# Other places for h's parts in the second half's row of operands, in an LSTM step on one core

## The chip, the core and the metric

The kernel runs on one core of a Trainium2 chip. The metric is the device time of one execution in microseconds (us). The core has TensorE (PE; its weight loads are shown apart as PEld), VectorE (DVE), ScalarE (ACT), GpSimd (POOL) and SyncE (SP); each works through its own queue in order and waits on semaphores that the others raise.

## The reference

One LSTM layer over a sequence, added to its input: 16 sequences (N), 512 steps (T), width 512 (D and H).

```python
xW = jnp.einsum('ntd,dg->ntg', x, Wx) + b
def step(carry, xw_t):
    prev_h, prev_c = carry
    a = xw_t + prev_h @ Wh
    i, f, o = sigmoid of a[:, :H], a[:, H:2H], a[:, 2H:3H];  g = tanh(a[:, 3H:])
    next_c = f * prev_c + i * g
    next_h = o * jnp.tanh(next_c)
    return ((next_h, next_c), next_h)
out = x + hs          # hs: the next_h of all steps; h0 = cond_1024, c0 = 0
```

The inputs are float32. Step t + 1 needs h of step t, so the loop over t can't be opened up.

## The kernel before

**Halves.** The hidden units are taken in two halves, a (h = 0) and b (h = 1). Each half has its own gates bank in PSUM, its own operand tiles and its own chain of elementwise work, and the two chains are interleaved so that TensorE has products of one half to do while the other half's gates are worked on.

**Products.** The product of h with Wh is made of float16 products. Wh is split once into three float16 tensors, `wq[0]`, `wq[1]` and `wq[2]`. In each step h is split into float16 parts that lie in one row of operands per half, `parts[h][t % 2]`, two times five slots of 16 columns (N): p1 is h scaled and rounded, copy is p1 once more, p2 is the remainder of h after p1, p2r is a second combination of the two. A product takes two neighbouring slots as its stationary operand of 32 columns, 16 of them for the main part of the sum and 16 for a part that is later divided by LO = 4096. Which of the two 16 rows has which meaning changes with the parity of t. There are three kinds: q1 (with `wq[0]`) takes p1 and p2, q2 (with `wq[1]`) takes copy and p2r, q3 (with `wq[2]`) takes p1 and a slot that stays zero. `products(t, i, kh, h)` issues one of them: qi for the half kh of h's rows and the half h of the gates, as eight matmuls of 128 x 32 weights against 256 columns, two contraction chunks (cc) times four column groups (j).

**Names.** "q3ba" is q3 with half b's operands into half a's gates. The order on TensorE is written out by hand in STEP_PE, and that on VectorE and ScalarE in STEP; every engine keeps exactly this order:

```python
STEP_PE = "q3aa q3ab q1ab q1aa q2aa q3ba q1ba q2ba q2bb q1bb q2ab q3bb x0 x1"
```

x0 and x1 are `project`, the float32 projections of a later pair of steps (L165).

**The chain of a half.** When the last product into gates a (q2ba) is done, turn_a and turno_a transpose the gates (L224), fold_a and foldo_a join the two parts (L231), ScalarE makes the tanh and sigmoids (L258, L260, L264), scale_a multiplies o's by a scale (L266), mix_a and cell_a make the new cell (L268, L274), ctanh_a its tanh (L276). Then come the parts: p1 on VectorE (L284), h on VectorE (L278), copy on ScalarE (L288, it reads p1), p2 on VectorE (L290), rem on VectorE (L294), p2r on VectorE (L298). Half b's chain is the same and begins after q3bb. `slots(t, h, kind)` gives where a part is written for step t + 1: kind 0 is p1, 1 is p2, 2 is copy, 3 is p2r.

**Around it.** `seed` puts the projection into the gates bank two steps ahead (ScalarE, L175), and every second step has the residual (L325 on VectorE, L326 on POOL) and the next transposition of x (L161).

Of the kernel before, what the change touches and what calls it, by code (L numbers as in the profile page):

```python
# [31 lines left out]
def lstm_residual(ctx: ExitStack, tc: tile.TileContext, x, h0, wx, wh, b, out):  # L32
# [78 lines left out]

    parts = [
        [const.tile([P, 2, 5 * N], HP, tag=f"parts{h}{i}", name=f"parts{h}{i}") for i in range(2)]
        for h in range(2)
# [65 lines left out]
    def products(t, i, kh, h):  # L182
        g = gates[h][t % 2]
        a = parts[kh][t % 2]
        k = ((1, 3, 0), (0, 3, 1))[t % 2][i - 1]
        for cc in range(2):
            for j in range(NJ):
                nc.tensor.matmul(  # L188
                    g[j * Q : (j + 1) * Q, :GU],
                    lhsT=a[:, cc, k * N : (k + 2) * N],  # L190
                    rhs=wq_j[i - 1][:, 2 * kh + cc, h, j],
                    start=False,
                    stop=False,
                    skip_group_check=True,
                )
# [43 lines left out]

    def slots(t, h, kind):  # L240

        k = ((1, 2, 3, 4), (1, 0, 4, 3))[(t + 1) % 2][kind]
        return parts[h][(t + 1) % 2][:, :, k * N : (k + 1) * N]

    def hl(t, h):
# [2 lines left out]
    def act(t, op, h):  # L248
# [22 lines left out]
        elif op == "cell":  # L271
            gc[h] = state.tile([P, 2, 2 * N], FP, tag=f"gc{h}", name=f"gc{h}_{t}")
            pr = v["pr", h]
            nc.vector.tensor_tensor(gc[h][:, 1], pr[:, 0], pr[:, 1], ALU.add)  # L274
        elif op == "ctanh":
            nc.scalar.activation(new("tch", t, h, [P, 2 * N]), gc[h][:, 1], AF.Tanh)  # L276
        elif op == "h":
            nc.vector.scalar_tensor_tensor(  # L278
                hl(t, h), two(v["os", h]), LO, two(v["tch", h]), ALU.mult, ALU.mult
            )  # L280
        elif t + 1 == T:
            return
        elif op == "p1":
            nc.vector.tensor_tensor(  # L284
                slots(t, h, 0), two(v["os", h]), two(v["tch", h]), ALU.mult
            )
        elif op == "copy":
            nc.scalar.copy(slots(t, h, 2), slots(t, h, 0))  # L288
        elif op == "p2":
            nc.vector.scalar_tensor_tensor(  # L290
                slots(t, h, 1), slots(t, h, 0), -LO, hl(t, h), ALU.mult, ALU.add
            )
        elif op == "rem":
            nc.vector.scalar_tensor_tensor(  # L294
                new("rem", t, h, [P, 2, N]), slots(t, h, 0), -LO, hl(t, h), ALU.mult, ALU.add
            )
        else:
            nc.vector.scalar_tensor_tensor(  # L298
                slots(t, h, 3), v["rem", h], 2.0, slots(t, h, 1), ALU.mult, ALU.subtract
            )  # L300
# [184 lines left out]
    for t in range(T):  # L485
# [5 lines left out]
        for op in STEP_PE.split():  # L491
            if op[0] == "x":
                if q < NP:
                    project(q, 2 * half + int(op[1:]))
            elif t:
                products(t, int(op[1]), "ab".index(op[2]), "ab".index(op[3]))
            elif op[1] == "3":
                first_products("ab".index(op[2]), "ab".index(op[3]), hT0)

        for op in STEP.split():  # L500
            name, h = op.split("_")
# [47 lines left out]
```

## Time and profile before

| | |
|---|---|
| median of 3 runs | 2294.73 us (2294.44 to 2298.69) |
| profiled execution | 2294.09 us |
| its span | 2291.7 us |
| granted TensorE clock | 0.999 |
| PE busy | 2249.4 us, 57445 matmuls |
| PEld busy | 1572.7 us |
| DVE, ACT, POOL busy | 1952.7, 1838.1, 127.2 us |
| products, L188 | 49056 matmuls, mean 273 ns each |
| projections, L165 | 8192 matmuls, mean 593 ns each |

The span is the profiled execution from its first to its last instruction. Matmuls are pipelined and the ends of them are modelled, so several are in flight at a time and the mean of one is not the time that it adds. PEld is the loading of weights, which goes on beside matmuls. The chain of waits is followed back from the last instruction: at each step to what released it, or to the instruction before it on its engine. An idle time is put down to what ended it. EVENT_SEMAPHORE is an instruction that only waits.

### The profile page before, as it was taken

The numbers are of one execution on the slowest core, as the hardware profiler recorded it, in microseconds if no ns is written. First come the engines' busy times: TensorE is split into PE (matmuls) and PEld (weight loads), VectorE is DVE, ScalarE is ACT, GpSimd is POOL, SyncE is SP. The second block draws the span as 40 slices with busy tenths as digits, with TensorE's granted clock in tenths as the row PEclk, the third lists the DMA queues.
The fourth block names the chain that finished last, engine by engine and source line by source line (L and its number), as shares of the span: only waits on it lengthen the run. The fifth ranks groups of instructions, "written<-read, shape, count | busy, mean of one in ns | idle before, by whom it ended". The sixth has DMA issues, their size and how long they took to land.

```text
span 2291.7 us, 137735 instructions
## 1 busy us (share of the span) xinstructions
PE 2249.4 (98%) x57445; PEld 1572.7 (69%) x57445; DVE 1952.7 (85%) x11813; ACT 1838.1 (80%) x7959; POOL 127.2 (6%) x281
## 2 busy tenths in 40 slices
PE   4999999999999999999999999999999999999997
PEld 2677766777766777777666777776677777666775
DVE  5888888888888888888888888888888888888887
ACT  5888888888888888888888888888888888888887
POOL 1000000000000000000000000000000000000000
PEclk9999999999999999999999999999999999999999
DMA  7000000100100001000001001010000010010000
GB/s 166 13 21 15 22 18 17 22 15 20 22 14 22 22 13 22 21 14 22 17 18 22 15 20 22 13 22 22 13 22 19 17 22 18 17 22 15 20 18 12
DMA packets 85005, 51.10 MB, mean 22 GB/s; under 512 B 17104, under 2 KB 82720, under 8 KB 83872
## 3 DMA queue, kind: packets, MB, share of 16 engines
q1 hardware_dynamic: 83008, 37.82, 7.6%
q8 instruction: 452, 7.41, 1.4%
q0 software_dynamic: 928, 2.37, 0.5%
q10 hardware_dynamic: 448, 2.13, 0.4%
q14 instruction: 169, 1.38, 0.2%
HBM read 25.47 MB, written 16.78 MB: 18 GB/s over the span
## 4 chain that ended last, share of the span: by engine, by line
PE 98%; DMA 2%; DVE 0%; issue 0%; ACTq 0%; POOLq 0%; POOL 0%; SPq 0%
PE gates L188 59%; PE xb L165 38%; DMA wh_sb<-in_L_cond_Wh_dram 1%; DMA xs<-in_x_dram 0%; DMA wx_sb<-in_L_cond_Wx_dram 0%; PE gates L201 0%; PE xb L374 0%; ACTq L134 0%; DVE gt L224 0%; DVE preo L231 0%; DVE pre L231 0%; DVE parts L284 0%; DVE gto L224 0%; POOLq L544 0%; POOL ob L326 0%
## 5 line engine op out<-in xcount | busy, mean ns | idle before, releaser
L188 PEld LDWEIGHTS <-parts 128*32 128x32 f16 x49056 | 1307.1, 96 | 368.8 <-DVE parts L284 298.8
L188 PE MATMUL gates<-wq,parts 128*32 128x256 f16 x49056 | 1449.2, 273 | 4.2 <-DVE parts L284 4.2
L165 PE MATMUL xb<-wx_sb,xT 128*32 128x512 f32 x8192 | 977.1, 593 | 22.5 <-DMA wx_sb<-in_L_cond_Wx_dram 22.5
L224 DVE STREAM_TRANSPOSE gt<-gates 128x192 f32<-128x192 f32 x1024 | 391.7, 383 | 229.9 <-PE gates L188 170.7
L165 PEld LDWEIGHTS xb<-wx_sb,xT 128*32 128x32 f32 x8192 | 264.6, 110 | 327.5 <-issue 303.5
L258 ACT ACTIVATE gc<-pre 128x32 f32<-128x32 f32 x1022 | 234.7, 230 | 274.7 <-DVE pre L231 261.9
L175 ACT ACTIVATE gates<-xb,mask 128x256 f32<-128x256 f32 x1024 | 450.3, 440 | 2.1 <-PE xb L165 2.1
L266 ACT ACTIVATE os<-so,sc 128x32 f32<-128x32 f32 x1024 | 329.1, 321 | 16.6
L288 ACT COPY parts<-parts 128x32 f16<-128x32 f16 x1022 | 214.4, 210 | 131.7 <-DVE parts L284 131.7
L231 DVE SCALAR_TENSOR_TENSOR pre<-gt 128x96 f32<-128x96 f32 x1024 | 253.6, 248 | 0.0
L260 ACT ACTIVATE sif<-pre 128x64 f32<-128x64 f32 x1024 | 245.7, 240 | 0.0
L326 POOL TENSOR_TENSOR ob<-hb,xs 128x128 f32<-128x128 f32 x256 | 117.1, 457 | 2146.0 <-DVE hb L325 1732.5
L224 DVE STREAM_TRANSPOSE gto<-gates 128x64 f32<-128x64 f32 x1024 | 229.6, 224 | 0.0
L276 ACT ACTIVATE tch<-gc 128x32 f32<-128x32 f32 x1024 | 226.8, 221 | 0.3
L298 DVE SCALAR_TENSOR_TENSOR parts<-rem,parts 128x32 f16<-128x32 f32 x1022 | 196.3, 192 | 35.5
L264 ACT ACTIVATE so<-preo 128x32 f32<-128x32 f32 x1024 | 226.4, 221 | 0.0
L231 DVE SCALAR_TENSOR_TENSOR preo<-gto 128x32 f32<-128x32 f32 x1024 | 192.6, 188 | 17.5
L290 DVE SCALAR_TENSOR_TENSOR parts<-parts,hist 128x32 f16<-128x32 f16 x1022 | 192.0, 188 | 17.7
L268 DVE TENSOR_TENSOR pr<-sif,gc 128x64 f32<-128x64 f32 x1022 | 204.2, 200 | 0.0
L284 DVE TENSOR_TENSOR parts<-os,tch 128x32 f16<-128x32 f32 x1022 | 196.5, 192 | 0.0
L274 DVE TENSOR_TENSOR gc<-pr 128x32 f32<-128x32 f32 x1024 | 192.1, 188 | 0.0
L278 DVE SCALAR_TENSOR_TENSOR hist<-os,tch 128x32 f32<-128x32 f32 x1024 | 188.7, 184 | 0.3 <-ACT tch L276 0.3
(47 smaller groups left out, 730.8 us busy)
## 6 DMA issues: line engine op xcount, KB each, us to landing
xs<-in_x_dram SPq DMA_DIRECT2D x512, 32.0 KB, 2.0
out_dram<-ob SPq DMA_DIRECT2D x504, 32.0 KB, 1.7
wh_sb<-in_L_cond_Wh_dram ACTq DMA_DIRECT2D x4, 512.0 KB, 13.4
wh_sb<-in_L_cond_Wh_dram SPq DMA_DIRECT2D x4, 512.0 KB, 13.1
wx_sb<-in_L_cond_Wx_dram POOLq DMA_DIRECT2D x8, 256.0 KB, 9.5
wx_sb<-in_L_cond_Wx_dram SPq DMA_DIRECT2D x8, 256.0 KB, 6.8
bias<-in_L_cond_b_dram POOLq DMA_DIRECT2D x8, 32.0 KB, 13.4
out_dram<-ob SPq DMA_DIRECT2D x8, 24.0 KB, 1.6
```

Source lines behind the costliest of these rows:

```text
L165: nc.tensor.matmul(xb[q % NXB][j * Q : (j + 1) * Q], lhsT=xT[q][:, c], rhs=wx_j[:, c, j], start=False, stop=(c == NK - 1), skip_group_chec ...
L175: nc.scalar.mul(gates[h][t % 2][:, :GU].rearrange("p (g u) -> p g u", g=G), xb[t // 2 % NXB].rearrange("p (g h u) -> p h g u", g=G, h=2)[: ...
L188: nc.tensor.matmul(g[j * Q : (j + 1) * Q, :GU], lhsT=a[:, cc, k * N : (k + 2) * N], rhs=wq_j[i - 1][:, 2 * kh + cc, h, j], start=False, st ...
L224: nc.vector.transpose(gt.rearrange("p b m -> p (b m)"), gates[h][t % 2][:, b0 * Q : b1 * Q])
L231: nc.vector.scalar_tensor_tensor(pre.rearrange("p g (c n) -> p (g c) n", c=2), gt[:, :, (1 - t % 2) * N : (2 - t % 2) * N], 1.0 / LO, gt[: ...
L258: nc.scalar.activation(gc[h][:, 0], v["pre", h][:, 0], AF.Tanh)
L260: nc.scalar.activation(new("sif", t, h, [P, 2, 2 * N]), v["pre", h][:, 1:3], AF.Sigmoid)
L264: nc.scalar.activation(new("so", t, h, [P, 2 * N]), v["preo", h][:, 0], AF.Sigmoid)
L266: nc.scalar.mul(new("os", t, h, [P, 2 * N]), v["so", h], S[h])
L268: nc.vector.tensor_tensor(new("pr", t, h, [P, 2, 2 * N]), v["sif", h], gc[h], ALU.mult)
L276: nc.scalar.activation(new("tch", t, h, [P, 2 * N]), gc[h][:, 1], AF.Tanh)
L288: nc.scalar.copy(slots(t, h, 2), slots(t, h, 0))
```

## The change

For half b the parts get other slots, and the products with half b's operands read from other slots. For half a everything stays. In terms of slots 0 to 4 of half b (the place that stays zero is written 0):

| | slots before | slots after | q1, q2, q3 begin at, before | after |
|---|---|---|---|---|
| operands of even t | 0, p1, p2, copy, p2r | p1, p2, 0, copy, p2r | 1, 3, 0 | 0, 3, 2 |
| operands of odd t | p2, p1, 0, p2r, copy | p2, p1, p2r, copy, 0 | 0, 3, 1 | 0, 2, 3 |

So q1 and q2 take the same pairs as before, and q3 of half b takes copy and the zero slot where it took p1 and the zero slot.

```diff
+    AT = (((1, 3, 0), (0, 3, 1)), ((0, 3, 2), (0, 2, 3)))
+    SLOTS = (((1, 2, 3, 4), (1, 0, 4, 3)), ((0, 1, 3, 4), (1, 0, 3, 2)))
...
     def products(t, i, kh, h):
         g = gates[h][t % 2]
         a = parts[kh][t % 2]
-        k = ((1, 3, 0), (0, 3, 1))[t % 2][i - 1]
+        k = AT[kh][t % 2][i - 1]
...
     def slots(t, h, kind):
 
-        k = ((1, 2, 3, 4), (1, 0, 4, 3))[(t + 1) % 2][kind]
+        k = SLOTS[h][(t + 1) % 2][kind]
         return parts[h][(t + 1) % 2][:, :, k * N : (k + 1) * N]
```

## The prediction

> **What bounds the kernel now.** I read the page first: busy shares, then the chain that ended last.
>
> ```profile
> PE 2249.4 (98%) x57445; PEld 1572.7 (69%) x57445; DVE 1952.7 (85%) x11813; ACT 1838.1 (80%) x7959; POOL 127.2 (6%) x281
> PE 98%; DMA 2%; DVE 0%; issue 0%; ACTq 0%; POOLq 0%; POOL 0%; SPq 0%
> PE gates L188 59%; PE xb L165 38%; DMA wh_sb<-in_L_cond_Wh_dram 1%; DMA xs<-in_x_dram 0%; DMA wx_sb<-in_L_cond_Wx_dram 0%; PE gates L201 0%; PE xb L374 0%; ACTq L134 0%; DVE gt L224 0%; DVE preo L231 0%; DVE pre L231 0%; DVE parts L284 0%; DVE gto L224 0%; POOLq L544 0%; POOL ob L326 0%
> ```
>
> The chain is TensorE alone: products (L188) and projections (L165). So time can only come from the spacing of matmuls, and VectorE (85%) and ScalarE (80%) matter only by when they release TensorE. Next the waits: which have TensorE on the left.
>
> ```profile
> PEld L188 <- DVE parts L284: 298.8, 511, 1.7
> DVE gt L224 <- PE gates L188: 170.7, 450, 0.6
> ACT parts L288 <- DVE parts L284: 131.7, 511, 0.3
> ```
>
> The 298.8 us are no lost time: that weight load is q3aa's, it starts 144 ns ahead of its matmul, and the last projections still stream. The second line says that the next step's transposes wait for TensorE: a step that gets shorter on TensorE pulls VectorE along.
>
> The list hides one thing. The groups of line 188 show it:
>
> ```profile
> L188 PEld LDWEIGHTS <-parts x49056: 91/97/98, 56.0 to 2283.6; 128*32 128x32 f16 x200
> L188 PEldq EVENT_SEMAPHORE  x1022: 51/51/51, 56.7 to 2282.6; - x171
> ```
>
> 1022 is two per step over the 511 steps t = 1 to 511. An instruction on TensorE's queue that must wait for two engines gets a separate semaphore instruction of 51 ns ahead of it. In the listing of both programs' waits these are q2aa's and q2ba's first weight loads, which wait for VectorE (p2r) and ScalarE (copy).
>
> Now one step, t = 277, in the timeline. A "quad" is four matmuls on four column groups; a call of products() is two quads. Columns: start, duration.
>
> ```profile
> 1261.01 0.22 ACT L288 COPY parts<-parts 128x32 f16<-128x32 f16 x1 [0.26 <-DVE parts L284]
> 1261.44 0.19 DVE L298 SCALAR_TENSOR_TENSOR parts<-rem,parts 128x32 f16<-128x32 f32 x1
> ...
> 1261.75 0.09 PEld L188 LDWEIGHTS <-parts 128*32 128x32 f16 x1
> ```
>
> These are copy_b, p2r_b, and q2ba's first load. Below, for each of four instants in that step, the matmuls in flight; the first column is the start of the oldest, so these are the starts of successive quads: q3ba's second, q1ba's two, q2ba's first.
>
> ```profile
> 1261.43 0.40 PE L188 MATMUL gates<-wq,parts 128*32 128x256 f16 x8
> 1261.54 0.41 PE L188 MATMUL gates<-wq,parts 128*32 128x256 f16 x8
> 1261.65 0.42 PE L188 MATMUL gates<-wq,parts 128*32 128x256 f16 x8
> 1261.78 0.40 PE L188 MATMUL gates<-wq,parts 128*32 128x256 f16 x8
> ```
>
> 0.11, 0.11, then 0.13 us. In the trace's exact starts, averaged over the steps, quads follow each other at 109.2 ns, except q2ba's first: 137.4 ns, 28.2 late. The four quads after it come 2.5 ns closer in sum. So q2ba costs 25.7 ns net in a step of 4362.6 ns, and nothing else in the step waits: the time from the last quad to the next step's first is 1826 ns, constant within 1 ns, with the four projection quads in it. The loads' busy time says the same of this step, quad by quad (PE, then PEld): the load queue is empty ahead of q2ba.
>
> ```profile
> 1261.54:1261.65 0.11, 0.11 (x13) 0.11 (x7) 0.11 (x2) 0.11 (x2) 0.00 (x0) 1.00 0.00 0
> 1261.65:1261.76 0.11, 0.11 (x12) 0.02 (x4) 0.11 (x1) 0.11 (x1) 0.00 (x0) 1.00 0.00 0
> ```
>
> **What is removed: q2ba's second wait.** q3 for b now reads the copy of p1 with an empty slot beside it, so q3ba's first load waits for ScalarE's copy_b, and q2ba's, two products later, needs only p2r_b. One wait is left on each, so 511 of the 1022 semaphore instructions should go. Price: q2ba's load now starts 117 ns after p2r_b's end (the semaphore instruction starts 41 after it, takes 51, and the load follows 25 later). A load with a single wait for VectorE starts 53 ns after the producer's end (q3aa after p1_a, in all steps). Load to matmul takes at least 30 to 31 ns (q2ba). New need: 53 + 31 = 84 ns after p2r_b. The undisturbed quad would come 148 - 28 = 120 ns after p2r_b. So the wait falls 36 ns inside its cover, and all 25.7 ns go: 511 x 25.7 = 13.1 us.
>
> **What is added: q3ba waits for copy_b, not p1_b.** p1_b ended 339 ns before q3ba's matmul; copy_b ends only 89 ns before (median; 85 at the 5th percentile). What is needed is ScalarE's signal to TensorE plus those 31 ns. The trace has no load released by ScalarE alone, so I bound it. By consumer, from producer's end to start: ScalarE after VectorE 33 to 35, VectorE after ScalarE 31, ScalarE after ScalarE 32, TensorE's load after VectorE 53, POOL after VectorE 78. The delay belongs to the consumer and ScalarE is some 2 ns quicker as producer, so I take 51, with 31 and 78 as ends. 51 + 31 = 82 against 89: covered, by 7 ns. If the cover is gone each ns costs 0.51 us: at 78 the stall is 20 ns, 10 us of the 13 lost; at 31 it is nothing.
>
> In 20 of the 511 steps half b is itself late by tens of ns (the first step, and some with other VectorE work ahead); there q3ba now pays where q2ba paid before, 1.4 us in sum. Behind the waiting load stand all later loads and matmuls of TensorE, q1ba first; q1ba's own operand p2_b (230 ns ahead) and q2ba's have more cover than q3ba, so a stall at q3ba replaces one at q2ba and does not add to it.
>
> [...]
>
> **At nothing.** The slots' other places change neither count, size nor order of instructions on VectorE, ScalarE, POOL and SP; the listing of their waits is the same. Loads take 91 to 98 ns at all offsets in use. The chain of half a starts at q2ba's end and returns at p1_a, so it moves up with q2ba; p1_a keeps 197 ns ahead of q3aa where 84 are needed. VectorE is idle 0.10 us or more before turn_a in nearly all steps, more than the 26 ns pulled. If that cover failed, q3aa would take up to those 26 ns back.
>
> **Sum.** 13.1 - 1.4 = 11.7 us. The profiled execution took 2294.09 us (span 2291.7, so 2.4 around it), 0.6 under the median of 2294.73: 2294.1 - 11.7 = 2282.4.
>
> **Rivals.**
> [...]
> 2. A slower signal from ScalarE, 58 to 78 ns: q3ba stalls up to 20 ns and the gain shrinks to between 11.7 and 2 us: 2283 to 2292. For it: no row of this pair. Against: ScalarE's signals are the quickest elsewhere.
> 3. No change, 2294: q2ba is late because p2r_b's signal is, not because of the semaphore instruction; or that instruction stays. For it: the load waited for both anyway. Against: 53 ns for q3aa and q1ba with one wait, and the listing, where q2ba is left with one.
>
> **How the numbers follow.** Forecast 0.74, rival 1 0.09, rival 2 0.10 (0.07 of it still over 0.2% faster), rival 3 0.05, and 0.02 for something slower unseen. 0.2%, 4.6 us, is about what a measurement of this kernel can tell from no change. Faster 0.81, same 0.08, slower 0.11. The range goes from 2279.5 (no loss in late steps, and runs a little under the profiled one) to 2291 (nearly the far end of rival 2), and leaves out rivals 1 and 3.
>
> **What would show it.** Right: semaphore instructions on line 188 fall to 511; q2ba's quad comes at 109 ns, its load 53 ns after p2r_b or later; the step is some 4338 ns; q3ba's load starts about 51 ns after copy_b and its quad still at 109 to 110. Wrong: a spacing at q3ba of 115 or more (rival 2), of some 168 (rival 1), or at q2ba of 137 as now (rival 3); or 1826 ns before q3aa grown.

## The result and the profile after

The changed kernel takes 2284.2 us (median of 6 runs, 2280.46 to 2285.3) beside 2295.66 us for the kernel before (6 runs): a ratio of 0.9943 (of the means), 95% interval 0.9931 to 0.9956. The forecast was 2282.4 us, between 2279.5 and 2291.

From the page of the changed kernel's profiled execution (2284.45 us, span 2282.3), its busy shares and its chain; all its line numbers are 4 higher than before:

```profile
PE 2239.7 (98%) x57445; PEld 1515.8 (66%) x57445; DVE 1952.7 (86%) x11813; ACT 1839.5 (81%) x7959; POOL 126.7 (6%) x281
PE 98%; DMA 2%; DVE 0%; issue 0%; ACTq 0%; POOLq 0%; POOL 0%; SPq 0%
```

The work is the same, instruction for instruction, and the bound is still TensorE. The groups of the product line (now 192), its load and its semaphore instruction:

```profile
L192 PEld LDWEIGHTS <-parts x49056: 92/97/97, 59.3 to 2273.7; 128*32 128x32 f16 x200
L192 PEldq EVENT_SEMAPHORE  x511: 51/51/51, 60.1 to 2271.9; - x171
```

Of the 1022 semaphore instructions 511 are left, q2aa's. Step t = 277 again, in the timeline: copy_b, q3ba's first load, p2r_b, q2ba's first loads.

```profile
1257.31 0.22 ACT L292 COPY parts<-parts 128x32 f16<-128x32 f16 x1 [0.26 <-DVE parts L288]
...
1257.58 0.09 PEld L192 LDWEIGHTS <-parts 128*32 128x32 f16 x1
...
1257.74 0.19 DVE L302 SCALAR_TENSOR_TENSOR parts<-rem,parts 128x32 f16<-128x32 f32 x1
...
1257.98 0.10 PEld L192 LDWEIGHTS <-parts 128*32 128x32 f16 x3
```

q3ba's load follows copy_b's end (1257.53) by 0.05 us, and q2ba's follows p2r_b's end (1257.93) by 0.05 where it was 0.12. Then the matmuls in flight at five instants, the first column again the start of a quad: q3ba's two, q1ba's two, q2ba's first.

```profile
1257.62 0.39 PE L192 MATMUL gates<-wq,parts 128*32 128x256 f16 x8
1257.73 0.39 PE L192 MATMUL gates<-wq,parts 128*32 128x256 f16 x8
1257.84 0.39 PE L192 MATMUL gates<-wq,parts 128*32 128x256 f16 x8
1257.95 0.39 PE L192 MATMUL gates<-wq,parts 128*32 128x256 f16 x8
1258.06 0.39 PE L192 MATMUL gates<-wq,parts 128*32 128x256 f16 x8
```

0.11 us throughout. In the trace's exact starts, the mean spacing is 109.2 ns for every quad of the step, q2ba's too, and 109.4 for q3ba's first. The step went from 4362.6 to 4337.0 ns. (These means, and those below, leave out the first step and the last three.)

**Where the time came from.** I cut the span at the first and the last product quad of the 511 steps: before 56.04 + 2227.60 + 8.04 us, after 59.40 + 2214.40 + 8.49. The loop gave 13.2 us; 3.4 were lost ahead of it and 0.4 behind it. The 3.4 us have nothing to do with slots. One stretch near the start, by stage (its length, then the busy time and count of PE, PEld, DVE, ACT and POOL, then the granted clock), in the profile of before:

```profile
50.00:57.00 7.00, 7.00 (x185) 5.11 (x186) 3.10 (x19) 3.53 (x15) 0.00 (x0) 1.00 0.01 2
```

and the same stretch in the profile of after:

```profile
50.00:57.00 7.00, 7.00 (x109) 5.14 (x111) 0.00 (x0) 1.41 (x3) 0.00 (x0) 0.53 0.01 2
```

In this execution of the changed kernel the granted clock was 0.50 from 49.7 to 56.5 us, and 6.8 us at half the clock are the 3.4. Its runs lie on two levels: 2280.46 and 2280.84 us with a granted clock of 0.999, 2284.2 to 2285.3 with 0.998. That this stretch makes the upper one is an estimate, from the 3.4 us here beside 3.4 to 4.8 between the levels. The kernel before has two levels as well (2294.44 to 2295.75 and 2298.29 to 2298.69 in these runs), and its profiled execution was one without the stretch. Level for level, by the means of these runs, the change is worth 14.5 us on the lower and 14.0 on the upper; the medians are only 11.5 apart because four of the six runs before lie on the lower level and two of the six after.

### The profile page after: what moved, and what is told of

The parts are those of the page before. It is cut to its first block, busy times and chain, and to the rows that moved or that the text cites. A ratio compares the mean times of both kernels' runs of the same rounds, so it can differ in the third digit from the quotient of the medians.

```text
span 2282.3 us, 137224 instructions
## 1 busy us (share of the span) xinstructions
PE 2239.7 (98%) x57445; PEld 1515.8 (66%) x57445; DVE 1952.7 (86%) x11813; ACT 1839.5 (81%) x7959; POOL 126.7 (6%) x281
## 3 DMA queue, kind: packets, MB, share of 16 engines
q8 instruction: 451, 7.39, 1.4%
## 4 chain that ended last, share of the span: by engine, by line
PE 98%; DMA 2%; DVE 0%; issue 0%; ACTq 0%; POOLq 0%; POOL 0%; SPq 0%
PE gates L192 59%; PE xb L169 39%; DMA wh_sb<-in_L_cond_Wh_dram 1%; DMA xs<-in_x_dram 0%; DMA wx_sb<-in_L_cond_Wx_dram 0%; PE gates L205 0%; PE xb L378 0%; ACTq L138 0%; DVE gt L228 0%; DVE preo L235 0%; DVE pre L235 0%; DVE parts L288 0%; DVE gto L228 0%; POOLq L548 0%; POOL ob L330 0%
## 5 line engine op out<-in xcount | busy, mean ns | idle before, releaser
L192 PEld LDWEIGHTS <-parts 128*32 128x32 f16 x49056 | 1265.0, 96 | 397.6 <-DVE parts L288 300.7
L192 PE MATMUL gates<-wq,parts 128*32 128x256 f16 x49056 | 1428.1, 273 | 4.2 <-DVE parts L288 4.2
L169 PEld LDWEIGHTS xb<-wx_sb,xT 128*32 128x32 f32 x8192 | 240.9, 110 | 344.7 <-issue 319.6
## 6 DMA issues: line engine op xcount, KB each, us to landing
wh_sb<-in_L_cond_Wh_dram ACTq DMA_DIRECT2D x4, 512.0 KB, 13.2
bias<-in_L_cond_b_dram POOLq DMA_DIRECT2D x8, 32.0 KB, 13.2
```

What stands on the lines that cost most here:

```text
L169: nc.tensor.matmul(xb[q % NXB][j * Q : (j + 1) * Q], lhsT=xT[q][:, c], rhs=wx_j[:, c, j], start=False, stop=(c == NK - 1), skip_group_chec ...
L192: nc.tensor.matmul(g[j * Q : (j + 1) * Q, :GU], lhsT=a[:, cc, k * N : (k + 2) * N], rhs=wq_j[i - 1][:, 2 * kh + cc, h, j], start=False, st ...
```

## The experiments

Theory A is the prediction's: the second wait of q2ba's load, with its semaphore instruction, was the loss. Theory B: the places themselves count. The further questions are how much cover q3ba has, what a late load costs, what the late steps are, and what the clock does at the start.

**1. Other places, q3 with p1 as before**

```diff
-    AT = (((1, 3, 0), (0, 3, 1)), ((0, 3, 2), (0, 2, 3)))
-    SLOTS = (((1, 2, 3, 4), (1, 0, 4, 3)), ((0, 1, 3, 4), (1, 0, 3, 2)))
+    AT = (((1, 3, 0), (0, 3, 1)), ((3, 0, 2), (2, 0, 3)))
+    SLOTS = (((1, 2, 3, 4), (1, 0, 4, 3)), ((3, 4, 0, 1), (3, 2, 1, 0)))
```

> Half b's parts lie in other places than before, but q3 still takes p1 (even steps: copy, p2r, 0, p1, p2; odd steps: p2r, copy, p2, p1, 0). Theory A (the second wait on q2ba's first load is what costs): q2ba keeps both waits, so nothing changes: 2294 to 2296 us beside the kernel before, ratio within 0.2% of 1; q2ba's first quad some 28 ns late in each step, 1022 semaphore instructions on the product line. Theory B (the places themselves, the offsets at which parts are written and read): as fast as the changed kernel, some 13 us less than before.

Ratio to before 0.9996 (0.9988 to 1.0004), 13 runs; q2ba's first quad comes after 137 ns in even steps and 141 in odd ones, and all semaphore instructions are still there:

```profile
L192 PEldq EVENT_SEMAPHORE  x1022: 51/51/51, 56.6 to 2283.2; - x171
```

So other places alone do nothing, and theory B falls as far as it can be tested: q3ba reads at the same offsets as in the changed kernel, but the change's places in full can't be had with q3 on p1, since the zero slot doesn't lie beside p1 there.

**2. The change in even steps alone**

```diff
-    AT = (((1, 3, 0), (0, 3, 1)), ((0, 3, 2), (0, 2, 3)))
-    SLOTS = (((1, 2, 3, 4), (1, 0, 4, 3)), ((0, 1, 3, 4), (1, 0, 3, 2)))
+    AT = (((1, 3, 0), (0, 3, 1)), ((0, 3, 2), (0, 3, 1)))
+    SLOTS = (((1, 2, 3, 4), (1, 0, 4, 3)), ((0, 1, 3, 4), (1, 0, 4, 3)))
```

> The change in the operands of even t alone; odd t as before. Theory A: half of the gain, 255 of 511 steps: 6.5 us less than before from the spacing of the quads, and some 766 or 767 semaphore instructions; within the one run q2ba's quad comes after 109 ns in even steps and after some 135 in odd ones. The single matmuls that came some 70 to 100 ns late just after q2ba in about 30 steps of the kernel before: if they come from the queue being held at q2ba, they stay in odd steps only, about 15; if they come from something with a beat of its own, they fall on both parities alike. Theory B: no half gain need appear.

Ratio 0.9969 (0.9958 to 0.998), half of the gain. The product line's group of semaphore instructions in this kernel:

```profile
L192 PEldq EVENT_SEMAPHORE  x767: 51/51/51, 56.7 to 2276.2; - x192
```

And from its timeline q1ba's two quads and q2ba's first, in flight as above, in the even step t = 276 and then in the odd step t = 277:

```profile
1253.79 0.41 PE L192 MATMUL gates<-wq,parts 128*32 128x256 f16 x8
1253.89 0.41 PE L192 MATMUL gates<-wq,parts 128*32 128x256 f16 x8
1254.00 0.41 PE L192 MATMUL gates<-wq,parts 128*32 128x256 f16 x8
...
1258.12 0.41 PE L192 MATMUL gates<-wq,parts 128*32 128x256 f16 x8
1258.23 0.43 PE L192 MATMUL gates<-wq,parts 128*32 128x256 f16 x8
1258.37 0.40 PE L192 MATMUL gates<-wq,parts 128*32 128x256 f16 x8
```

0.11 us in the even step, 0.14 in the odd one; in the means 109.2 and 140.0 ns. One kernel, one clock, the same work: the loss goes where the second wait goes. The guess on the late steps missed: not 15 of them were left but 2.

**3. The change for half a too**

```diff
-    AT = (((1, 3, 0), (0, 3, 1)), ((0, 3, 2), (0, 2, 3)))
-    SLOTS = (((1, 2, 3, 4), (1, 0, 4, 3)), ((0, 1, 3, 4), (1, 0, 3, 2)))
+    AT = (((0, 3, 2), (0, 2, 3)), ((0, 3, 2), (0, 2, 3)))
+    SLOTS = (((0, 1, 3, 4), (1, 0, 3, 2)), ((0, 1, 3, 4), (1, 0, 3, 2)))
```

> The same change for half a too: q3aa, the first product of the step, takes copy_a. In the changed kernel copy_a ends 46 ns after q3aa's first matmul starts. By the prediction's way of costing (51 ns from ScalarE's end to the load, 31 to the matmul) q3aa comes 46 + 81 = 127 ns later in each step, and nothing takes it back: 4337 + 127 = 4464 ns a step, 65 us more than the changed kernel, about 2348 us; 0 or 1 semaphore instructions a step are left, with no gain from it, as q2aa's was covered. Rival (a late operand at the step's start is absorbed, since p1_a has over 100 ns to spare and the other chain gains time): less than 30 us more than the changed kernel.

2336.5 us, ratio 1.0173 (1.0157 to 1.0188): slower, with no semaphore instruction left at all. The sign was right, the size too large: the step is 4443.5 ns, 106.5 more than the changed kernel's, not 127. From the waits of this kernel:

```profile
PEld L192 <- ACT parts L292: 428.2, 511, 1.9
```

And from the timeline of one of its steps copy_a, q3aa's load and q3aa's first quad:

```profile
1285.96 0.20 ACT L292 COPY parts<-parts 128x32 f16<-128x32 f16 x1
...
1286.21 0.09 PEld L192 LDWEIGHTS <-parts 128*32 128x32 f16 x1 [0.83 <-ACT parts L292]
1286.21 0.40 PE L192 MATMUL gates<-wq,parts 128*32 128x256 f16 x8
```

The load comes 51 ns after copy_a's end as costed, but the matmul comes 1 to 2 ns after the load, not 31; the quad after it then takes 119.5 ns instead of 109.2. 96.5 + 10.4 makes the 107.

**4 to 6. The changed kernel with copy_b held back**

```diff
         elif op == "copy":
+            if h == 1:
+                nc.scalar.copy(pad[:, :n], bias[:, :n])    # n = 320, 380, 440
             nc.scalar.copy(slots(t, h, 2), slots(t, h, 0))
```

> The changed kernel with one more ScalarE instruction ahead of copy_b in each step (a copy of 128 x 320 float32 into a tile that nobody reads), so that copy_b comes later by some D; by the rows of ScalarE copies I expect D of 30 to 90 ns. The changed kernel's copy_b ends 97 ns ahead of q3ba's matmul, and 81 to 82 are needed: 15 ns of cover. Theory (load hidden, each ns past the cover costs its ns): q3ba is D - 15 late, the step longer by that, 0.51 us for each ns: for D = 60, 45 ns and 23 us, so some 2307 us. Rival (the load itself is exposed once it is late, 97 ns in the path): a jump of 97 ns more, 73 us for the same D. A third possibility, that the stall is taken back at q2ba, which has some 45 ns to spare: no loss up to D = 60.

> As the last one of this kind, with 380 instead of 320 columns in the extra ScalarE copy. With 320 it took 442 ns and ended just where copy_b could start, so copy_b was not late at all. At 0.72 ns a column (from 320 to the 512 columns that take 580) it takes 485, and copy_b is 43 ns late: its end plus 50 is 1088 ns after q3aa's start, the quad is due at 1092. Theory (31 ns from load to matmul always): q3ba's quad 27 ns late, 14 us more than the changed kernel: 2298. Rival (a load that comes late is exposed with its 97 ns): 93 ns late, 47 us more. Rival (taken back at q2ba): no loss.

> The same with 440 columns: some 528 ns, copy_b 86 ns late, so that the load starts at 1131 ns, when the array has already run dry at 1092. By 31 ns from load to matmul always: q3ba 70 ns late, 36 us more than the changed kernel: 2320. By what both halves' trace shows for q3aa (the array dry: the matmul 1 ns after its load, the next quad 10 ns longer): 40 + 10 = 50 ns, 26 us more: 2310. By the exposed load: 137 ns late, 70 us more.

| n | extra copy, ns | copy_b later by | load, before (-) or after the quad is due | q3ba's two quads | step | median us, ratio to before |
|---|---|---|---|---|---|---|
| none | | | -47 | 109.4, 109.2 | 4337.0 | 2284.2, 0.9943 |
| 320 | 442 | 0 | -47 | 109.5, 109.2 | 4337.0 | 2284.38, 0.9946 (0.9933 to 0.996) |
| 380 | 492 | 43 | -4 | 109.8, 117.8 | 4345.6 | 2286.67, 0.9946 (0.9929 to 0.9962) |
| 440 | 542 | 92 | +45 | 157.0, 119.7 | 4395.0 | 2311.25, 1.0057 (1.0042 to 1.0072) |

The first told nothing of q3ba: the extra copy fitted into ScalarE's idle time before copy_b, which it did show to be free. The second should have cost 27 ns a step by the 31 ns from load to matmul, and cost 8.6 (its loop took 2219.0 us instead of 2214.4; the ratios, from four runs each, do not resolve that). The third, in the timeline: the extra copy, copy_b, q3ba's load, then the quads q2aa's second and q3ba's two.

```profile
1269.12 0.54 ACT L294 COPY pad<-bias 128x440 f32<-128x440 f32 x1
1269.56 0.21 ACT L295 COPY parts<-parts 128x32 f16<-128x32 f16 x1
...
1269.83 0.09 PEld L193 LDWEIGHTS <-parts 128*32 128x32 f16 x1 [0.15 <-ACT parts L295]
...
1269.67 0.45 PE L193 MATMUL gates<-wq,parts 128*32 128x256 f16 x8
1269.83 0.40 PE L193 MATMUL gates<-wq,parts 128*32 128x256 f16 x8
1269.95 0.39 PE L193 MATMUL gates<-wq,parts 128*32 128x256 f16 x8
```

Load and quad at 1269.83, and 0.12 us to the next: 48 + 10.5 = 58 ns a step, 29.6 us, nearer to the 50 of "1 ns, then 10" than to the 70 of "31 always" and far from 137. Nothing is taken back at q2ba. It also shows what the change stands on: with copy_b 92 ns later its whole gain is lost.

**7 and 9. The changed kernel with full-row fillers before the first step**

```diff
             for _ in range(16):
-                zeros(xb[3], False)
+                nc.tensor.matmul(
+                    xb[3], lhsT=wq[0][:, 0, :P], rhs=wq[0][:, 0, : G * P],
+                    start=False, stop=False, skip_group_check=True,
+                )
```

> The changed kernel, with the 16 filler matmuls before the first step (one row of zeros against 512 columns) replaced by 16 of 128 rows of real data, into a bank that is overwritten afterwards. The changed kernel's runs lie at 2280.5 to 2280.8 (granted clock 0.999) and at 2284.2 to 2285.3 (0.998), and its profile shows half clock from 49.7 to 56.5 us, under this filler and the first products. [...] Then all runs of this kernel lie near 2280.5, clock 0.999, with no half-clock stretch at 50 us. Rival: the filler's rows don't matter: both levels again, 2 or more of 6 runs near 2284.

> The changed kernel with the 16 fillers of 128 rows once more. [...] Rival (the four runs at 2280 before were chance): a third to two thirds of the runs at 2284.

2280.81 us (2279.79 to 2281.09, 4 runs), ratio 0.9922 (0.9907 to 0.9937), and again 2281.29 (2280.43 to 2281.9, 5 runs), ratio 0.9921 (0.9907 to 0.9934): one level, for the second at the upper end of the 2280 to 2281 forecast and a little over, clock 0.999 in all nine. The new fillers differ from the old in two things, 128 rows for one and real data for zeros, and no run tells which of the two counts, or by what the clock is granted. The same stretch as above, of the second of them:

```profile
50.00:57.00 7.00, 7.00 (x153) 4.60 (x154) 2.72 (x14) 3.54 (x13) 0.00 (x0) 1.00 0.01 2
```

**8. The changed kernel again, beside the fillers**

> The changed kernel again, on one chip with the fillers. Two levels as in its first runs, some 2280.6 (granted clock 0.999) and some 2284.4 (0.998), the same ones apart as in the kernel before (2294 to 2296 and 2298 to 2300); ratio to before about 0.994.

2284.34 us (2282.34 to 2284.79, 5 runs), ratio 0.9932 (0.992 to 0.9945). Three runs near 2284.5 and two at 2282.4, so the gap is smaller here than the 4 us expected; the fillers are worth about 3 us at the median.

**10. The kernel before with full-row fillers** (the same edit as in 7)

> The kernel before with the same 16 fillers of 128 rows. If filler and change act apart from each other: one level, 2293.5 to 2295.5, some 13 to 14 us above the changed kernel with these fillers, and no runs at 2298 to 2300.

One level, 2296.86 to 2298.29 us in 11 runs, clock 0.999, but 2297.15 at the median and not 2294.5: the kernel before varies in its steps as well. Against the kernel before with its own fillers the ratio is 0.9993 (0.9984 to 1.0001), so for this kernel a gain from the fillers is not shown. Its loop took 2230.2 us here and 2227.6 in the first profile. The traces show where: p2r_b ends 1413 ns after q3aa's start here (median) and 1407 there, and q2ba's quad follows after 142.9 ns instead of 137.4. In the changed kernel p2r_b's end moves too, from 1398 to 1403 ns between profiles, but there it is covered, and the loop took 2214.4 us in all four profiles of it (after, 7, 8, 9). With equal fillers the change is worth 2297.15 - 2281.29 = 15.9 us.

**11. The kernel before with 20 of its own fillers**

```diff
-            for _ in range(16):
+            for _ in range(20):
                 zeros(xb[3], False)
```

> The kernel before with 20 instead of 16 of its own fillers: all instructions of TensorE after them stand 8 places later, nothing else changes. The profile of before has some 23 steps in which a quad at q2ba is 30 ns or more later than in its neighbours (steps 43, 171, 299 and 427, 128 apart, among them). If that comes from the place of an instruction in the stream (its fetching), most of these go to other steps; if from something else of those steps, they stay in the same ones. The time says little: 1 to 3 us more for the fillers.

2300.74 us in its one run. With steps counted from 0 as there, 17 steps have a quad at q2ba that is about 30 ns or more late. Ten stand exactly 60 steps after a late step of the kernel before (103, 231, 359 and 487 for 43, 171, 299 and 427), five more 60 steps after one when counted modulo 128; the other two, 196 and 452, are in every profile but experiment 3's, those of the changed kernel too. The 60 agrees with an estimate from the instruction stream. The page's instruction queue line of before is

```profile
q8 instruction: 452, 7.41, 1.4%
```

7.41 MB in 452 packets is 16.4 KB each. No view says whose queue it is; the changed kernel, with 511 instructions fewer on TensorE, has 451 packets and 7.39 MB there. Taken as the queue of TensorE's some 116,000 instructions, it is 64 bytes an instruction, so 256 to a packet. A step has 226: 112 matmuls with a load each, and two semaphore instructions. By this estimate 128 steps are exactly 113 packets, and 60 steps are 53 packets less 8 instructions, the 8 by which the fillers moved the stream.

In the timeline of before, step 332 (t = 333): p2r_b, q2ba's first load, then q1ba's second quad and q2ba's first.

```profile
1505.81 0.19 DVE L298 SCALAR_TENSOR_TENSOR parts<-rem,parts 128x32 f16<-128x32 f32 x1
...
1506.12 0.09 PEld L188 LDWEIGHTS <-parts 128*32 128x32 f16 x1
...
1506.02 0.30 PE L188 MATMUL gates<-wq,parts 128*32 128x256 f16 x4
1506.32 0.29 PE L188 MATMUL gates<-wq,parts 128*32 128x256 f16 x4
```

The load comes 0.12 us after p2r_b's end, as in every step; the matmuls come 0.20 us after the load. The first matmul that comes late is q2ba's first in steps 204, 332 and 460, its second in 187 and 315, its third in 42, 170, 298 and 426, its fourth in 25, 281 and 409, and so on through q2ba's second quad: for each matmul one number modulo 128. 17 steps on it is one matmul earlier, and by the same estimate 17 steps are 15 packets and two instructions, a load and its matmul. In experiments 1 and 10, also with 226 instructions to a step, each matmul that comes late has the same number as here (one step, 331 in experiment 1, excepted); in experiment 11 each has the number that lies 60 further. So by the estimate a step can be late where one place of a packet falls at one of the eight matmuls behind q2ba's wait; it is not late each time, and what is at that place, a packet's boundary or something else, no run shows.

## Why the prediction was right, point by point

- **What is removed.** Right: 511 semaphore instructions gone, q2ba's load 52 ns after p2r_b's end (53 forecast), its quad at 109.2 ns; experiments 1 and 2 tie the gain to that wait. Its median step fell from 4360 to 4337 ns, 23 x 511 = 11.8 us of the loop's 13.2. The cover left is larger than the 36 ns costed (q2ba's load starts 78 ns ahead of its matmul), because the 30 ns from load to matmul go with the semaphore instruction: with it 30 again in experiment 2's odd steps, without it 2 to 4 at the median in experiments 3, 5 and 6. The trace of before could have told: behind q2ba's first matmul, the other three of the quad follow their loads by 1 to 3 ns. The first step of before (t = 1) has the 30 too, with a single wait: q1ba's first load 53 ns after p2_b's end, its matmul 30 ns after the load, and its quad 110 ns behind the one before. I read it as a minimum; it only showed a matmul that waited for its turn:

```profile
57.31 0.10 PEld L188 LDWEIGHTS <-parts 128*32 128x32 f16 x4
57.34 0.40 PE L188 MATMUL gates<-wq,parts 128*32 128x256 f16 x8
```

- **What is added.** Right: q3ba's load 50 ns after copy_b, where I had taken 51 from the other pairs of engines without a row of this one. copy_b itself ended 97 ns ahead of its matmul, not 89, and against copy_b the load came 68 ns later than before, not 66. By the costed 82 the cover was 15 ns; by experiments 5 and 6 it is over 40.
- **The late steps**, booked as a loss of 1.4 us. Wrong in sign: the step that failed is "there q3ba now pays where q2ba paid before". I took all 20 for half b coming late from outside. In six it does (the first, the last three, 196 and 452), and there q3ba pays, 69 to 121 ns, where q2ba had paid 87 to 151. In the other 14 half b was late because q2ba had been late one step earlier, where by the estimate of experiment 11 that place of a packet met the held queue; none of these is left, and of the 23 late steps that experiment 11 counts in the kernel before 21 are gone. The 25.7 ns are a mean that already held their excess, so nothing was to be taken off: 13.1 against the loop's 13.2.
- **The sum.** 11.7 forecast; 13.2 from the loop, less 3.4 ahead of it and 0.4 behind it in the profiled execution. The clock was no term of the sum; the first profile had no such stretch, though its three runs (2294.44 to 2298.69) already lay on both levels. Without it the loop alone gives 2294.1 - 13.2 = 2280.9, the level of the better runs. That 11.7 comes so near the 11.5 us between the medians is luck in part: without the wrong term the forecast was 13.1, level for level the runs give 14.0 to 14.5, and it is the unequal shares of the two levels that bring the medians to 11.5.
- **At nothing.** Right: 1826 ns before q3aa as before, VectorE and ScalarE as busy as before, p1_a ends 207 ns ahead of q3aa.
- **The rivals.** Rival 1, a load at q3ba that is not hidden, did not come. Its 168 ns hold a stall of 59 ns that no run shows: q3ba's quad came after 109.4 ns, with the load 50 ns after copy_b. A load 47 ns ahead of its quad is covered, and one 4 ns ahead costs 9 ns, not its own 97 (experiments 4 and 5). PEld is busy 66% of the span beside a PE of 98%, so loads do go on beside matmuls here; by what means, no run shows. A slower signal from ScalarE: 50 ns, no. No change: 767 semaphore instructions with half the gain rule it out.

What stays open: why experiment 2, which keeps the second wait in its odd steps, has none of the late steps but 196 and 452, which speaks against that place of a packet behind such a wait being enough by itself; what makes those two late; and why p2r_b comes some 6 ns later in some profiles of the kernel before.

The fastest version run is the change with full-row fillers, 2280.8 to 2281.3 us: 0.9921 of the time before.

## What to carry to other kernels

Where an instruction of TensorE waits for two other engines, look for the extra semaphore instruction: here there were 1022 of 51 ns, and the list of waits showed none of them. If one of the two operands is already needed, or could be used, a little earlier in that queue where there is slack, let that earlier instruction wait for it. Cost the new place by its own cover, engine by engine: the same edit won 13 us for half b and lost 52 for half a.

## What the runs showed of the hardware

- A semaphore instruction on TensorE's queue cost more than its 51 ns: q2ba's load came 117 ns after p2r_b's end with it (before) and 52 without (after), and where no earlier matmul was left to start the matmul came 30 ns after its load with it (before, and experiment 2's odd steps) and 2 to 4 without (experiments 3, 5 and 6).
- A weight load that was late by a little cost less than its 97 ns: with the load 4 ns ahead of the due quad the step grew by 8.6 ns (experiment 5), with it 45 ns behind by 58 (experiment 6), and in experiment 3 the matmul followed its load by 1 to 2 ns and only the next quad was 10 ns longer.
- Where every step has the second wait (before, 1, 10 and 11), single steps were some 30 to 170 ns late behind it (the kernel before), at numbers that repeat after 128 steps, which agrees with packets of 16.4 KB by the estimate in experiment 11; with the wait in odd steps alone (experiment 2) none was, but for 196 and 452.
- With sixteen fillers of one row of zeros before the first step the granted clock of the changed kernel was 0.998 in four of six runs and 0.999 in two, and in one profile 0.53 in a stretch with TensorE busy all the time (7.00 of 7.00 us); with 128 rows of real data no half-clock stretch of 6.8 us stands ahead of the loop in the three profiles, and the granted clock is 0.999 in all 20 runs of the two kernels.
